# A cross-network kernel: first factors by TensorE, products on GpSimd, four head chunks, M read by quarters

## The chip, the cores and the metric

The kernel runs on one core of one Trainium2 chip. TensorE multiplies matrices into PSUM, VectorE (DVE in the profile) and GpSimd (POOL) work elementwise, ScalarE (ACT) applies functions and copies, and transfers are issued from the queues of SyncE (SP) and ScalarE. The metric is the device time of the whole kernel in microseconds (us).

## The reference

The input x has 1024 samples, 64 fields f and 16 components e. Three layers are formed, each from products of x with the layer before:

```python
z = einsum('bfe,bge->bfge', x0, h)          # all products of fields
y = einsum('oc,bce->boe', W[i], z) + b[i]   # 128 outputs
# layers 0 and 1: first 64 outputs are kept, last 64 become the next h
# layer 2: all 128 outputs are kept
out = sum_e(concat(kept)) @ fc_w.T + fc_b   # one number a sample
```

Because the last step is linear, the kernel never forms layer 2. With V2 = the row fc_w of layer 2 times W2 (64 x 64), and M = V2 applied to the last 64 outputs of W1 (a 64 x 64 x 64 tensor), layer 2 gives, for each sample and e, the sum over o of h1[o] times q[o], where h1 is the last half of layer 0 and q[o] is the sum over f and f' of M[f, f', o] x[f] x[f']. Both h1 and q are quadratic forms of the same products of x. The kept halves of layers 0 and 1 come in through small matrices called v0 and v1.

## The kernel before

**Tiles.** The samples are cut into 32 chunks of 32 samples, 512 columns each. The products of x with itself make 16 tiles of 128 rows by 512 columns, tile t = 4 j + i. Tile (j, i) is xa (the rows shifted by i) times xb (the rows shifted by 4 (j + 1), by 16 more in the lower half). `product(c, j)` makes the four tiles of one j in one VectorE instruction, 2048 elements in each partition, into a z tile. One last tile holds squares and x itself.

**Weights.** `w_all` holds, for each tile, 64 columns for h1, 64 for q, and 64 for h1 again. A full chunk takes 16 matmuls with 128 weight columns (`contract`), a product of q and h1 on VectorE (`factors`), and a sum over e (`sums`).

**Head chunks.** M is not an input: it is computed on the chip from W2 (w2s, pv, pt, v2t) and W1 (w1s, pm), copied to m_sb, written to DRAM (md) and read back along diagonals into ms. Until then only h1 can be computed. The chunks in `HEAD` therefore go through TensorE in two parts: part 0 (h1, kept in hb by `keep_h1`), and part 1 (q) when M is there. Each part multiplies 64 weight columns with the two halves of a chunk side by side (`half_contract`). The list is [4, 5, 6, 0, 1]; the products of 4, 5 and 6 are made a second time for part 1, those of the last two (`KEPT`) stay in their buffers.

**Shared last tiles.** From chunk `FIRST` = 8 on, four chunks share what follows their 16 tiles: `contract_shared` adds the squares, the v1 term and the v0 term (ys, two PSUM tiles for two pairs of chunks). Chunks below `FIRST` have a last tile each (`contract_last`), and the v0 term of a pair comes from `v0x(k)`. VectorE then multiplies it with x in `x_v0x(k)`.

**Order.** The schedule is by hand: every engine runs its instructions in the order in which the program writes them. In the main loop, turn s first loads chunk s + 2 of `order` and makes its products, then contracts chunk s, then has factors and sums of chunks before. Before the loop stand the preparation of v1 and v0 (`weigh`, two VectorE instructions of 2048 elements each).

**Buffers.** z tiles: 12 (three chunks). xa and xb: 3 each. PSUM [...]by tag: acc 4, y 2, set 2. A new tile of a tag waits until all uses of the tile that it replaces are done.

**Transfers.** Chunk loads, weights and most of M's reads are issued in order on SP; a share of M's writes and reads on ScalarE's queue.

Of the kernel before, what the change touches and what calls it, by code (L numbers as in the profile page):

```python
# [41 lines left out]
F = 64  # L42
# [6 lines left out]
NI = 4  # L49
# [4 lines left out]
HEAD = [4, 5, 6, 0, 1]  # L54
# [3 lines left out]
FIRST = 8  # L58
# [4 lines left out]
def cin_kernel(ctx, tc, xra, xrb, xh, wh, w0r, w1h, w2t, wx1, wx0, vec, out):  # L63
# [33 lines left out]

    pick = const_tile("pick", [128, 4])
# [14 lines left out]
    bd = const_tile("bd", [128, 128])  # L113
    nc.gpsimd.memset(w_all[:, NT, :], 0.0)
    nc.gpsimd.memset(bd, 0.0)


    xas, xbs, zls, xxs = {}, {}, {}, {}
# [12 lines left out]
    def load_chunk(c):  # L131
        load_xa(c)
        xb = xp.tile([128, NJ, N], F32, tag="xb", name=f"xb_{c}")
        nc.sync.dma_start(out=xb, in_=xrb[c])
        xbs[c] = [xb[:, j, :] for j in range(NJ)]

    c0, c1, c2, c3, c4 = HEAD
    xb0 = z_tile("xb0")
# [3 lines left out]
    load_xa(c0, slice(0, 2))  # L142
    nc.sync.dma_start(out=xb0[:, 0, :], in_=xh)
    load_xa(c0, slice(2, 4))
    nc.sync.dma_start(out=w0t[:, 0, :], in_=wh)
    nc.sync.dma_start(out=xb0[:, 1:NJ, :], in_=xrb[c0][:, 1:NJ, :])
    nc.sync.dma_start(out=w0t[:, 1:NJ, :], in_=w0r)
    xbs[c0] = [xb0[:, j, :] for j in range(NJ)]
    w0s = [w0t[:, j, :].rearrange("p (i v g) -> p i v g", v=2, g=F) for j in range(NJ)]
    load_chunk(c1)  # L150
    for k in range(2):
        nc.sync.dma_start(out=w2s[k], in_=w2t[k])
    load_chunk(c2)
    nc.sync.dma_start(out=w1s, in_=w1h)
# [17 lines left out]
    def product(c, j, pieces=1):  # L172
        zs[c, j] = z_tile(f"z_{c}_{j}")
        n = NI // pieces
        for i in range(0, NI, n):
            nc.vector.tensor_tensor(  # L176
                zs[c, j][:, i : i + n, :], xas[c][:, i : i + n, :],
                xbs[c][j].unsqueeze(1).to_broadcast([128, n, N]), ALU.mult,
            )
        if j == NJ - 1:  # L180
            nc.scalar.activation(zs[c, j][SQ, 0, :], xas[c][SQ, 0, :], AF.Square)  # L181
# [5 lines left out]
    def last_tile(c):  # L187

        if c < FIRST:
            squares(c)  # L190
            nc.scalar.copy(zls[c][64:128], xas[c][64:128, 0, :])  # L191
        else:
            if c % 4 == 0:
                zls[c // 4] = xp.tile([128, N], F32, tag="zl", name=f"sq_{c}", bufs=4)
            at = 32 * (c % 4)
            nc.scalar.activation(zls[c // 4][at : at + 32], xas[c][0:32, 0, :], AF.Square)  # L196
        if c % 2 == 0:
            xxs[c // 2] = sp.tile([128, N], F32, tag="xx", name=f"xx_{c}", bufs=4)
        to = halves[c % 2]
        nc.scalar.copy(xxs[c // 2][to], xas[c][to, 0, :])  # L200
# [3 lines left out]

    def pieces(c):

        return parts[c] if c in parts else [(accs[c], slice(0, N))]

    def contract(c, j, piece=0):
        acc_c, cols = pieces(c)[piece]  # L210
        for i in range(NI):
            t = j * NI + i
            nc.tensor.matmul(  # L213
                acc_c, w_all[:, t, w_cols(c)], zs[c, j][:, i, cols],
                start=(t == 0 and (c < FIRST or c % 4 < 2)),
                stop=(t == NT - 1 and c >= FIRST and c % 4 >= 2),
            )

    def contract_last(c):
        nc.tensor.matmul(accs[c], w_all[:, NT, 0:128], zls[c], start=False, stop=True)  # L220

    def contract_shared(first):

        for r in range(4):
            c, at = first + r, slice(32 * r, 32 * r + 32)
            for acc_c, cols in pieces(c):
                nc.tensor.matmul(  # L227
                    acc_c, w_sq[at, w_cols(c)], zls[first // 4][at, cols], start=(r >= 2),
                    stop=(r < 2), tile_position=(32 * r, 0),
                )  # L230
        for k in (first // 2, first // 2 + 1):
            ys[k] = ps.tile([128, N], F32, tag="y", name=f"y_{k}")
            for n in range(2):
                c, rows, q = 2 * k + n, halves[n], halves[1 - n]
                for acc_c, cols in pieces(c):
                    nc.tensor.matmul(  # L236
                        acc_c[q], v1w[rows], xxs[k][rows, cols], start=False, stop=(c % 4 < 2),
                        skip_group_check=True,
                    )
            for rows in halves:  # L240
                nc.tensor.matmul(ys[k][rows], bd[rows, rows], xxs[k][rows], start=True, stop=True)  # L241
# [3 lines left out]
    def half_contract(c, part, j):  # L245

        cols = slice(part * F, (part + 1) * F)
        rows = slice(0, F) if part == 0 and j == NJ else slice(0, 128)
        for t in (NT,) if j == NJ else range(j * NI, (j + 1) * NI):
            z = zls[c] if t == NT else zs[c, j][:, t % NI, :]  # L250
            for n in range(2):
                nc.tensor.matmul(  # L252
                    accs[c][halves[n]], w_all[rows, t, cols], z[rows, n * H2 : (n + 1) * H2],
                    start=(t == 0), stop=(t == NT),
                )
# [9 lines left out]
    def factors(c, which=slice(0, 1)):  # L265
# [9 lines left out]
        h = halves[c % 2 if c >= FIRST else 0]  # L275
# [23 lines left out]
    def h1_weights(j):  # L299
        nc.vector.tensor_tensor(  # L300
            w_all[:, j * NI : (j + 1) * NI, 0:64], w0s[j][:, :, 0, :], w0s[j][:, :, 1, :], ALU.add
        )
# [4 lines left out]
    for j in range(NJ):  # L307
        product(c0, j, 2 if j == 0 else 1)
        if j == NJ - 1:
            nc.vector.memset(w0s[j][SQ, 0, 1, :], 0.0)  # L310
        h1_weights(j)
    nc.vector.tensor_copy(w_all[0:32, NT, 0:64], w0ds[0:32])
    for j in range(NJ + 1):
        half_contract(c0, 0, j)
    keep_h1(c0)
    squares(c1)
    load_chunk(c3)

# [12 lines left out]


    new_acc(c1, H2)
    for j in range(NJ - 1):
        product(c1, j)
    for j in range(2):
        half_contract(c1, 0, j)
# [6 lines left out]
    product(c1, NJ - 1)  # L344
    half_contract(c1, 0, 2)
    load_chunk(c4)
# [11 lines left out]
    for m in range(NI):  # L358
        nc.scalar.copy(m_sb[:, m, :], pms[m])  # L359

    for j in range(3, NJ + 1):
        half_contract(c1, 0, j)
# [29 lines left out]
    def head(c):  # L392
        new_acc(c, H2)
        for j in range(NJ):
            product(c, j)
        for j in range(NJ + 1):
            half_contract(c, 0, j)
        keep_h1(c)

    head(c2)  # L400


# [7 lines left out]
    for half in range(2):  # L410
        (nc.sync, nc.scalar)[half].dma_start(
            out=ms[halves[half], 0].rearrange("p (j i) g -> p j (i g)", i=NI),
            in_=skewed(16 * half + 4, 0, [[4 * row, NJ], [1, NI * F]]),
        )
    for i in range(NI):
        for half in range(2):
            queue = nc.scalar if half and i < 2 else nc.sync
            queue.dma_start(
                out=ms[halves[half], 1].rearrange("p (j i) g -> p j i g", i=NI)[:, :, i, :],
                in_=skewed(i, 16 * half + 4, [[4 * F, NJ], [1, F]]),  # L420
            )
# [4 lines left out]
    head(c3)  # L426


    new_acc(c4, H2)
    for j in range(NJ - 1):  # L430
        product(c4, j)
        half_contract(c4, 0, j)
    nc.vector.tensor_tensor(w_all[:, 0:NT, 64:128], ms[:, 0], ms[:, 1], ALU.add)
    nc.vector.tensor_copy(w_all[SQ, (NJ - 1) * NI, 64:128], dg[SQ])
    nc.vector.tensor_copy(w_all[0:32, NT, 64:128], w_sq[0:32, 64:128])
    product(c4, NJ - 1)
    load_chunk(2)
    w1x = flat_tile("w1x")
    nc.sync.dma_start(out=w1x, in_=wx1)
# [3 lines left out]
    for j in range(NJ - 1, NJ + 1):  # L443
        half_contract(c4, 0, j)
    keep_h1(c4)
    new_acc(c4, H2)
    for j in range(NJ):
        half_contract(c4, 1, j)
# [9 lines left out]
    last_tile(2)  # L458
    for j in range(NJ):
        product(2, j)  # L460
# [10 lines left out]
    load_chunk(3)  # L471
# [19 lines left out]
    last_tile(3)  # L491
    for j in range(NJ):
        product(3, j)
# [23 lines left out]
    order = list(range(2, NCH))  # L517
    first, last = slice(0, NP - 1), slice(NP - 1, NP)
    for s, c in enumerate(order):
        k, shared = c // 2, c >= FIRST  # L520
# [6 lines left out]
        if not shared or c % 4 < 2:  # L527
            new_acc(c, H2 if c in HEAD else N)
        for j in range(NJ):
            if j == 2:  # L530
# [5 lines left out]
                if c % 2 and not shared:  # L536
                    v0x(k)
            if c in HEAD:
                half_contract(c, 1, j)
            else:  # L540
                contract(c, j)
        if c in HEAD:
            half_contract(c, 1, NJ)
        elif not shared:
            contract_last(c)
# [8 lines left out]
        elif not shared or c % 4 in (0, 3):  # L554
            factors(order[s - 1])
        elif c % 4 == 2:
# [3 lines left out]
            x_v0x(k)  # L560
        if s == 1:
            x_v0x(0)
            sums(0)
        if c % 2 and not shared:
            x_v0x(k)
        elif s and c % 2 == 0:
            sums(k - 1)
# [89 lines left out]
```

## Time and profile before

| what | value |
|---|---|
| device time, median of 3 runs (lowest, highest) | 500.45 us (500.45, 500.82) |
| span of the profiled execution | 498.6 us |
| TensorE busy | 483.2 us, 97% |
| VectorE busy | 382.3 us, 77% |
| ScalarE busy | 92.7 us, 19% |
| GpSimd busy | 1.4 us |
| DMA | 82.80 MB, mean 166 GB/s |
| TensorE, full chunks (line 213) | 896 records, 374.2 us |
| TensorE, head chunks (line 252) | 640 records, 74.1 us |
| products (line 176) | 141 instructions, 315.1 us, mean 2271 ns |

An fp32 matmul leaves two records. Timeline lines give the start, the duration, the engine, the line of the code, the operation, what is written and read, the count of instructions merged, and in brackets the idle time before and what ended it. In lines of waits the waiting instruction stands left of the arrow, then come the total, the number of times and the longest. Lines of the chain give a start, a duration and the work.

### The profile page before, as it was taken

The page shows a single profiled execution, that of the slowest core. Times are in us where ns is not written, and L with a number is a line of the kernel's source. Part 1 is how long each engine was busy: PE and PEld are TensorE (multiplying, and loading weights), DVE is VectorE, ACT ScalarE, POOL GpSimd, SP SyncE. Part 2 cuts the span into 40 slices and gives each one's busy share as a digit, 9 for nine tenths or more (in the row PEclk, how much of TensorE's full clock was granted, in tenths as well). Part 3 has the DMA queues.
Part 4 walks back from the last instruction along what each step waited for, and adds up shares of the span by engine and source line. Part 5 has one row for each costly group of instructions (what it writes and reads, how often), then busy time and mean ns, then how long its engine had stood idle before and what let it go on. Part 6 is the DMA issues. An engine that isn't in the chain of part 4 may idle for free.

```text
span 498.6 us, 4414 instructions
## 1 busy us (share of the span) xinstructions
PE 483.2 (97%) x1850; PEld 229.3 (46%) x1850; DVE 382.3 (77%) x235; ACT 92.7 (19%) x160; POOL 1.4 (0%) x14
## 2 busy tenths in 40 slices
PE   3899999999999999999999999999999999999996
PEld 1455654456444344443444434443444434444474
DVE  4999799988999889798777686776877777771311
ACT  1243033122111121322011121110111120110001
POOL 1000000000000000000000000000000000000000
PEclk9999999999999999999999999999999999999999
DMA  8997895253454444456144442333444431000000
GB/s 328 425 418 227 335 423 212 108 231 135 181 229 183 170 174 162 168 179 256 71 169 170 168 168 104 114 138 150 168 170 168 163 120 55 0 0 0 2 0 0
DMA packets 14788, 82.80 MB, mean 166 GB/s; under 512 B 3789, under 2 KB 4461, under 8 KB 5233
## 3 DMA queue, kind: packets, MB, share of 16 engines
q1 hardware_dynamic: 13644, 81.24, 41.5%
q10 hardware_dynamic: 1124, 1.29, 0.9%
q8 instruction: 14, 0.23, 0.2%
q14 instruction: 6, 0.04, 0.0%
HBM read 80.88 MB, written 1.64 MB: 165 GB/s over the span
## 4 chain that ended last, share of the span: by engine, by line
PE 91%; DMA 5%; ACT 1%; SPq 0%; ACTq 0%; issue 0%; DVE 0%
PE acc L213 75%; PE acc L252 11%; DMA w1s<-in_w1h 4%; PE acc L236 2%; DMA xb<-in_xrb 1%; PE acc L227 1%; PE y L285 1%; PE acc L220 1%; PE po L507 0%; PE pm L354 0%; ACT zl L185 0%; ACT zl L191 0%; ACT m_sb L359 0%; ACT xx L200 0%; ACTq L378 0%
## 5 line engine op out<-in xcount | busy, mean ns | idle before, releaser
L213 PE MATMUL acc<-z,w_all 128*128 128x512 f32 (+1 forms) x896 | 374.2, 578 | 0.0
L176 DVE TENSOR_TENSOR z<-xa,xb 128x2048 f32<-128x2048 f32 (+1 forms) x141 | 315.1, 2271 | 50.7 <-PE acc L213 39.5
L213 PEld LDWEIGHTS acc<-z,w_all 128*128 128x128 f32 x896 | 169.4, 190 | 202.1 <-issue 200.0
L252 PE MATMUL acc<-z,w_all 128*64 128x256 f32 x640 | 74.1, 387 | 10.7 <-DVE w_all L300 9.1
L181 ACT ACTIVATE z<-xa 32x512 f32<-32x512 f32 x35 | 21.9, 626 | 323.6 <-DVE z L176 323.6
L279 DVE SCALAR_TENSOR_TENSOR uu<-acc,vs,q 64x512 f32<-64x512 f32 (+1 forms) x28 | 20.5, 731 | 61.5 <-ACT q L278 61.3
L252 PEld LDWEIGHTS acc<-z,w_all 128*64 128x64 f32 x640 | 45.6, 139 | 39.1 <-DVE w_all L300 10.3
L278 ACT COPY q<-acc 64x512 f32<-64x512 f32 (+1 forms) x28 | 15.8, 564 | 36.4 <-PE acc L213 22.9
L292 DVE TENSOR_REDUCE acc<-uu 128x64 f32<-128x1024 f32 (+3 forms) x19 | 20.3, 1073 | 0.4
L200 ACT COPY xx<-xa 64x512 f32<-64x512 f32 x32 | 19.6, 613 | 0.4
L196 ACT ACTIVATE sq<-xa 32x512 f32<-32x512 f32 x24 | 15.1, 628 | 0.6
L241 PE MATMUL y<-xx,bd 64*64 64x512 f32 x48 | 11.7, 604 | 0.0
L288 DVE SCALAR_TENSOR_TENSOR uu<-y,cx,xx 128x512 f32<-128x512 f32 x16 | 11.4, 745 | 0.3
L236 PE MATMUL acc<-xx,v1w 64*64 64x512 f32 (+1 forms) x50 | 11.6, 584 | 0.0
L227 PE MATMUL acc<-sq,w_sq 32*128 32x512 f32 (+1 forms) x50 | 6.8, 620 | 0.0
L185 ACT ACTIVATE zl<-xa 64x512 f32<-64x512 f32 x11 | 6.8, 624 | 0.1
L236 PEld LDWEIGHTS acc<-xx,v1w 64*64 64x64 f32 x50 | 3.1, 132 | 7.5 <-issue 7.4
L252 PE MATMUL acc<-zl,w_all 64*64 64x256 f32 (+1 forms) x40 | 6.1, 393 | 0.0
L258 ACT ACTIVATE hb<-acc,vs 128x256 f32<-128x256 f32 x5 | 2.4, 474 | 19.6 <-PE acc L252 19.6
L191 ACT COPY zl<-xa 64x512 f32<-64x512 f32 x8 | 4.9, 616 | 0.1
L227 PEld LDWEIGHTS acc<-sq,w_sq 32*128 32x128 f32 x50 | 2.2, 183 | 4.6 <-issue 4.5
L271 DVE TENSOR_TENSOR uu<-acc,hb 64x256 f32<-64x256 f32 x10 | 4.2, 421 | 0.2
(52 smaller groups left out, 51.0 us busy)
## 6 DMA issues: line engine op xcount, KB each, us to landing
xa<-in_xra SPq DMA_DIRECT2D x34, 1024.0 KB, 4.8
xb<-in_xrb SPq DMA_DIRECT2D x34, 1024.0 KB, 7.0
w<-in_w2t SPq DMA_DIRECT2D x2, 1024.0 KB, 13.4
xa<-in_xra SPq DMA_DIRECT2D x2, 512.0 KB, 4.0
w1s<-in_w1h SPq DMA_DIRECT2D x1, 1024.0 KB, 20.5
w1x<-in_wx SPq DMA_DIRECT2D x1, 1024.0 KB, 8.7
w0x<-in_wx SPq DMA_DIRECT2D x1, 1024.0 KB, 10.4
xb<-in_xrb SPq DMA_DIRECT2D x1, 768.0 KB, 6.8
```

Source lines behind the costliest of these rows:

```text
L176: nc.vector.tensor_tensor(zs[c, j][:, i : i + n, :], xas[c][:, i : i + n, :], xbs[c][j].unsqueeze(1).to_broadcast([128, n, N]), ALU.mult,)
L181: nc.scalar.activation(zs[c, j][SQ, 0, :], xas[c][SQ, 0, :], AF.Square)
L196: nc.scalar.activation(zls[c // 4][at : at + 32], xas[c][0:32, 0, :], AF.Square)
L200: nc.scalar.copy(xxs[c // 2][to], xas[c][to, 0, :])
L213: nc.tensor.matmul(acc_c, w_all[:, t, w_cols(c)], zs[c, j][:, i, cols], start=(t == 0 and (c < FIRST or c % 4 < 2)), stop=(t == NT - 1 and ...
L227: nc.tensor.matmul(acc_c, w_sq[at, w_cols(c)], zls[first // 4][at, cols], start=(r >= 2), stop=(r < 2), tile_position=(32 * r, 0),)
L236: nc.tensor.matmul(acc_c[q], v1w[rows], xxs[k][rows, cols], start=False, stop=(c % 4 < 2), skip_group_check=True,)
L241: nc.tensor.matmul(ys[k][rows], bd[rows, rows], xxs[k][rows], start=True, stop=True)
L252: nc.tensor.matmul(accs[c][halves[n]], w_all[rows, t, cols], z[rows, n * H2 : (n + 1) * H2], start=(t == 0), stop=(t == NT),)
L278: nc.scalar.copy(q[h, cols], acc_c[64 - h.start : 128 - h.start])
L279: nc.vector.scalar_tensor_tensor(uu[:, cols], acc_c[h], bh1[h], q[h, cols], ALU.add, ALU.mult)
L292: nc.vector.tensor_reduce(acc[rows, of, k, half], uus[k][rows, of, E * half.start : E * half.stop].rearrange("p k (b e) -> p k b e", e=E), ...
```

## The change

- **First chunk.** `HEAD` becomes [2, 3, 0, 1] and `FIRST` 4. The first chunk's xb is no longer loaded: TensorE makes its four shifted copies from xa's tile 0 with a 0/1 matrix `shift`, built on GpSimd by three affine_selects, into PSUM tiles of tags y, y, set and acc. Six matmuls on zeros run before. xa's first load is one tile, then three.
- **Operands in PSUM.** The second factors of the first two chunks, and one operand of two weight sums (w0p), lie in PSUM. ScalarE makes the copies (`to_psum`).
- **GpSimd** makes one z tile of the first chunk (j = 1) and one of the second (j = 3).
- **Order of loads.** w1s is loaded before the third chunk. Chunk 4 is loaded behind M's reads.
- **Order of work.** The second chunk's quarters run j = 0, 3, 1, 2 among the M work. In j = 3 tile 0 comes last. m_sb is filled in the order 0, 2, 1, 3.
- **M.** ms is read in 16 transfers by quarters (12 on SP, 4 on ScalarE's queue), where there were 10; the q columns of `w_all` are summed quarter by quarter (`q_weights`), and part 1 of chunk 0 begins after the first.
- **Loop.** The order is [4, 5, 6, 7, 2, 3, 8, ...]. Chunks 4 to 7 share their last tiles; `contract_last` is gone. `sums` is called at other places. w1x lies in the buffer of ms.

```diff
-HEAD = [4, 5, 6, 0, 1]
+HEAD = [2, 3, 0, 1]
-FIRST = 8
+FIRST = 4
...
+    pw = ps.tile([128, 128], F32, tag="y", name="pw")
+    for k in range(6):
+        nc.tensor.matmul(pw, bd, bd, start=True, stop=True)
+    shift = const_tile("shift", [128, 96])
+    nc.gpsimd.memset(shift, 0.0)
+    for base in (0, 64, -64):
+        nc.gpsimd.affine_select(
+            out=shift, in_=shift, compare_op=ALU.not_equal, fill=1.0, base=base,
+            pattern=[[-1, 96]], channel_multiplier=1,
+        )
...
-    load_xa(c0, slice(0, 2))
-    nc.sync.dma_start(out=xb0[:, 0, :], in_=xh)
-    load_xa(c0, slice(2, 4))
+    load_xa(c0, slice(0, 1))
+    load_xa(c0, slice(1, 4))
     nc.sync.dma_start(out=w0t[:, 0, :], in_=wh)
-    nc.sync.dma_start(out=xb0[:, 1:NJ, :], in_=xrb[c0][:, 1:NJ, :])
     nc.sync.dma_start(out=w0t[:, 1:NJ, :], in_=w0r)
-    load_chunk(c1)
+    load_xb(c1)
+    load_xa(c1)
     for k in range(2):
         nc.sync.dma_start(out=w2s[k], in_=w2t[k])
+    nc.sync.dma_start(out=w1s, in_=w1h)
     load_chunk(c2)
-    nc.sync.dma_start(out=w1s, in_=w1h)
...
+    xbs[c0] = [
+        ps.tile([128, N], F32, tag=tag, name=f"xp_{c0}_{j}", bufs=4 if tag == "acc" else 2)
+        for j, tag in enumerate(("y", "y", "set", "acc"))
+    ]
+    for j in (0, 2):
+        for r in range(2):
+            for h in range(2):
+                at = 4 * (j + r + 1) + 16 * h
+                nc.tensor.matmul(
+                    xbs[c0][j + r][halves[h]], shift[halves[r], at : at + F],
+                    xas[c0][halves[r], 0, :], start=True, stop=True,
+                )
...
-        for i in range(NI):
+        for i in tiles(j):
...
     new_acc(c0, H2)
     squares(c0)
-    for j in range(NJ):
-        product(c0, j, 2 if j == 0 else 1)
-        if j == NJ - 1:
-            nc.vector.memset(w0s[j][SQ, 0, 1, :], 0.0)
-        h1_weights(j)
     nc.vector.tensor_copy(w_all[0:32, NT, 0:64], w0ds[0:32])
+    product(c0, 0, 0, 1)
+    product(c0, 0, 1, NI)
+    nc.scalar.copy(xb0, xbs[c0][1])
+    xbs[c0][1] = xb0
+    product(c0, 1, engine=nc.gpsimd)
+    w0p = ps.tile([128, 2, NI, F], F32, tag="set", name="w0p")
+    for j in range(2):
+        nc.scalar.copy(w0p[:, j], w0s[j][:, :, 1, :])
+    h1_weights(0, w0p[:, 0])
+    product(c0, 2)
+    h1_weights(1, w0p[:, 1])
+    h1_weights(2)
+    nc.vector.memset(w0s[3][SQ, 0, 1, :], 0.0)
+    h1_weights(3)
+    for j, tag in enumerate(("y", "y", "acc")):
+        xbs[c1][j] = to_psum(xbs[c1][j], tag, f"xp_{c1}_{j}")
+    product(c0, 3)
     for j in range(NJ + 1):
         half_contract(c0, 0, j)
+    for j in range(NJ - 1):
+        product(c1, j)
+    product(c1, NJ - 1, engine=nc.gpsimd)
     keep_h1(c0)
     squares(c1)
     load_chunk(c3)
...
-    for half in range(2):
-        (nc.sync, nc.scalar)[half].dma_start(
-            out=ms[halves[half], 0].rearrange("p (j i) g -> p j (i g)", i=NI),
-            in_=skewed(16 * half + 4, 0, [[4 * row, NJ], [1, NI * F]]),
-        )
-    for i in range(NI):
+    for j in range(NJ):
         for half in range(2):
-            queue = nc.scalar if half and i < 2 else nc.sync
+            queue = nc.scalar if half and j < 2 else nc.sync
+            to = ms[halves[half]].rearrange("p v (j i) g -> p v j i g", i=NI)
             queue.dma_start(
-                out=ms[halves[half], 1].rearrange("p (j i) g -> p j i g", i=NI)[:, :, i, :],
-                in_=skewed(i, 16 * half + 4, [[4 * F, NJ], [1, F]]),
+                out=to[:, 0, j], in_=skewed(16 * half + 4 * (j + 1), 0, [[1, NI * F]])
+            )
+            queue.dma_start(
+                out=to[:, 1, j], in_=skewed(0, 16 * half + 4 * (j + 1), [[row, NI], [1, F]])
             )
...
-    head(c3)
-    new_acc(c4, H2)
+    load_chunk(FIRST)
+    keep_h1(c2)
+    new_acc(c3, H2)
+    for j in range(NJ):
+        product(c3, j)
+        if j == 2:
+            q_weights(0)
     for j in range(NJ - 1):
-        product(c4, j)
-        half_contract(c4, 0, j)
-    nc.vector.tensor_tensor(w_all[:, 0:NT, 64:128], ms[:, 0], ms[:, 1], ALU.add)
+        half_contract(c3, 0, j)
+    new_acc(c2, H2)
+    half_contract(c2, 1, 0)
+    for j in range(NJ - 1, NJ + 1):
+        half_contract(c3, 0, j)
+    keep_h1(c3)
+    for j in range(1, NJ):
+        q_weights(j)
...
+    last_tile(FIRST)
+    for j in range(NJ):
+        product(FIRST, j)
+    w1x = set_tile("w1x")
+    nc.sync.dma_start(out=w1x, in_=wx1)
+    for j in range(1, NJ):
+        half_contract(c2, 1, j)
     new_acc(c3, H2)
     for j in range(NJ):
         half_contract(c3, 1, j)
...
-    order = list(range(2, NCH))
+    order = [4, 5, 6, 7, 2, 3] + list(range(8, NCH))
...
-        if not shared or c % 4 < 2:
+        if head or c % 4 < 2:
...
-        elif not shared:
-            contract_last(c)
         elif c % 4 == 1:
             for n in (1, 2):
                 new_acc(c + n)
             contract_shared(c - 1)
...
         if s == 1:
             x_v0x(0)
             sums(0)
```

## The prediction

> **What bounds the kernel now.** I read the page's shares and slices first, then the timelines of TensorE, VectorE and the SP queue, then the chain. The profiled execution has a span of 498.6 us; its device time was 500.42, so I add 1.85 us to a span (the other runs: 500.45 to 500.82).
>
> ```profile
> PE 483.2 (97%) x1850; PEld 229.3 (46%) x1850; DVE 382.3 (77%) x235; ACT 92.7 (19%) x160; POOL 1.4 (0%) x14
> ...
> PE   3899999999999999999999999999999999999996
> ...
> DVE  4999799988999889798777686776877777771311
> ```
>
> TensorE is the bound nearly everywhere, but in the first 14 slices (170 us) VectorE is about as full as TensorE. There a delay of VectorE can reach TensorE.
>
> ```profile
> 8.35 3.56 PE L252 MATMUL acc<-z,w_all 128*64 128x256 f32 x16 [8.35 <-DVE w_all L300]
> 12.10 1.95 PE L252 MATMUL acc<-z,w_all 128*64 128x256 f32 x16 [0.20 <-DVE w_all L300]
> ```
>
> TensorE starts at 8.35; its first quarter (one j of a head chunk) takes 3.56, the next ones 1.95. After 40.35 it never waits until the tail.
>
> ```profile
> 104.80 10.94 PE acc L252 x100
> ...
> 143.82 27.46 PE acc L213 x64
> 171.29 1.07 PE acc L227 x8
> ```
>
> From these lines of the chain: a record of a head chunk costs 10.94 / 100 = 0.109, so one part of 64 records 7.0, with its last tile 7.44. A full chunk is 27.46 / 2 = 13.73. The shared end of four chunks (L227, L236, L241) runs from 171.29 to 174.24: 2.95.
>
> ```profile
> 58.76 8.90 DVE L176 TENSOR_TENSOR z<-xa,xb 128x2048 f32<-128x2048 f32 x4 [3.14 <-DMA xb<-in_xrb]
> 67.57 2.29 DVE L454 TENSOR_TENSOR w1x<-w1x,vs 128x2048 f32<-128x2048 f32 x1
> ...
> 87.29 8.90 DVE L176 TENSOR_TENSOR z<-xa,xb 128x2048 f32<-128x2048 f32 x4
> 96.22 1.75 DVE L271 TENSOR_TENSOR uu<-acc,hb 64x256 f32<-64x256 f32 x4
> 97.99 8.90 DVE L176 TENSOR_TENSOR z<-xa,xb 128x2048 f32<-128x2048 f32 x4
> ...
> 108.86 0.73 DVE L288 SCALAR_TENSOR_TENSOR uu<-y,cx,xx 128x512 f32<-128x512 f32 x1
> ```
>
> The reader is to see one unbroken chain: from the landing of the first full chunk (58.76) VectorE runs through the products of four chunks and two weighings to x_v0x(0), done at 109.6. TensorE's next use of that y buffer is v0x(2), at 115.67, so nothing waits for it now.
>
> ```profile
> SPq L123 <- ACT z L181: 60.4, 6, 13.4
> ```
>
> This line of SP's waits shows the rule of the buffers: a tile in a used slot waits for the last reader of the tile before it (here a chunk load for ScalarE's last read of an older xa).
>
> ```profile
> 43.79 0.65 SPq L411 DMA_DIRECT2D ms<-md  x1
> 44.49 5.11 SPq L418 DMA_DIRECT2D ms<-md  x6
> 49.65 0.61 SPq L423 DMA_DIRECT2D dg<-md  x1
> 50.74 0.59 SPq L424 DMA_DIRECT2D w_sq<-md  x1
> 51.45 0.40 SPq L123 DMA_DIRECT2D xa<-in_xra  x1
> ```
>
> M's reads hold SP from 43.79 to 51.33; the chunk load behind them starts at 51.45, its second half is issued at 51.90 and lands 6.7 later, at 58.6. That is what releases the VectorE chain above.
>
> **What the Trainium skill says.** "SBUF — State Buffer", Who interferes with whom: a VectorE instruction with at most one SBUF input does not contend with GpSimd. So a factor in PSUM lets GpSimd multiply beside VectorE; no run here shows it yet, POOL now only sets memory. "PSUM — Partial Sum Buffer", Engine vs sequencer instructions: VectorE's and ScalarE's queues are strict FIFO. The trace agrees: x_v0x(0) starts at 108.86, behind chunk 5's products, as written. "TensorE: Matmul & The Clock Gate", Part 1: after an idle window of about 3.4 us the array runs at half rate until it was busy about as long; 3.56 against 1.95 agrees. Price: "GPSIMD Engine Reference", 3.1, gives 4497 ns for an fp32 tensor_tensor of 2048 elements.
>
> **The change, part by part.**
>
> *Loads.* Landings now fit 3.6 us plus bytes at 0.41 MB per us (wh 7.4, w0r 11.3). By that, afterwards: xa's first quarter about 4.4, its rest 6.3, wh 7.0, w0r 8.9, the second chunk 13.9, w2 18.9, w1s 21.5 (now 9.41 + 20.5 = 29.9). Ahead of the third chunk 1 MB leaves (xb of the first) and 1 MB enters (w1s), so it still releases VectorE at 27.46. The fourth takes the place of now 17.47 + 14.9 = 32.4.
>
> *First chunk.* The eight shift matmuls have the shape of L354 (16 records, 1.95 us). The three affine_selects are not in the trace: 0.1 us each like POOL's memsets at the low end, 2 us at the high. Behind them in POOL's queue stands the memset of w_all, for which VectorE's first copy waits. I take all as done by 4.4. Then: product of tile 0 from about 5.8, three tiles until 8.4, h1_weights(0) 8.85. So TensorE starts at 8.9, no earlier than now, but warm from the dummy matmuls (gain 0 to 1.6). GpSimd's product starts after ScalarE's copy (6.9) and ends at 11.4. A PSUM operand costs little (0.745 for 512 elements in L288), so I keep 2.21 per product: VectorE is done at 14.7, and TensorE at 17.4 (now 20.0).
>
> *Second chunk.* TensorE: four quarters 7.0, last tile 0.58, pv 2.2, pt 1.9, pm 1.9, to 31.0; pm ends at 28.6, and M is copied by 30.0 (now 33.54). VectorE ends at 21.5 and idles until 27.46, so what GpSimd saves it here is not used. GpSimd's product (13.9 to 18.4) is hidden behind this chunk's first quarter and pv.
>
> *M.* Its writes are issued from 30.0 to 32.8, with the fourth chunk ahead until 32.4. Now they ended 2.4 after the load ahead of them (41.4 to 43.79); a shorter overlap makes it 3.4: 35.8 (bounds 34.8, last issue plus 2, and 38). Reads: SP issues 12 in place of 7, then dg and w_sq. Issues back to back repeat every 0.66, so 14 take 9.2; now, with waits for earlier reads, nine took 7.54, 0.84 each, so 11.7. I take that one: 47.5. ScalarE's four stand behind chunk 0's last square (37.0), two of them for q_weights(0), there about 43.4; VectorE comes there at 42.95 (27.46 + 7 x 2.21), and behind it waits one product. The last quarter, near 51, is needed at 52.2. TensorE is held by VectorE's 42.95; from there one quarter 1.75, chunk 0's second-part quarter 1.75, the last quarter and tile 2.35, three quarters 5.25, a part 7.0, the small pcx and pc 0.4, less 0.04 of rounding: full chunks can start at 61.4 (now 72.4).
>
> The load of chunk 4 is queued on SP behind all 14: issued at 47.5, landed 7.15 later (as from 51.45 to 58.6), so 54.7; 52.2 without the waits between reads.
>
> *Work of TensorE.* One head chunk (15.0), three full chunks with a last tile (3 x 14.6) and two v0x (1.7), 60.5 in all, become a group of four: 2 x 27.46 + 2.95 = 57.9. Saved: 2.6. From 61.4 without waits: chunk 4 with the kept chunks' last tiles 14.95, chunk 5 with v0x 14.6, shared end 2.95: 93.9. Behind it: 6 and 7 27.46; second parts of 2 and 3 7.44 + 8.49 (one v0x); 8 and 9 27.66; shared 2.95; and 498.6 - 174.24 = 324.4 as now: 398.4. Without a new wait the span would be 492.3.
>
> *The new wait.* Turn s=1 is now a single chunk; afterwards it is chunk 5, which ends in contract_shared(4) with two new y tiles. Tag y has two PSUM buffers (bufs=2 of pool ps). v0x(0) of the same turn holds one until x_v0x(0), which is written behind this turn's products of chunk 7. So the second y waits on VectorE's queue, and every later chunk of TensorE is behind it. VectorE from 54.7: products of chunk 4 8.9, weighing and copies 5.4, chunk 5 8.8, weighing and copies 5.5, chunk 6 8.9, factors of the kept two 1.8, chunk 7 8.9, x_v0x 0.75; sum 49.0, so 103.7. The accumulators of 6 and 7, which wait for those factors (94.0), are free earlier. The last group of the shared end takes 0.9: 104.6. TensorE, there about 95.8, idles 7.9. A cold array after it costs 0 to 1.7; I take 1.6, the excess at the start now, since the idle is over twice 3.4. Span 104.6 + 398.4 + 1.6 = 504.6, time 506.4. Later turns are covered: chunk 8's products end near 140, TensorE comes to it at 148.
>
> *At nothing:* the tile order in j=3 (chunk 3's square of 0.63 is hidden by three tiles), sums moved (VectorE ahead of TensorE there), w1x in the set buffer (lands about 58, used at 63.6), sqs apart (names only).
>
> **Rivals.**
> A, *no wait for y*, the slot being free sooner or VectorE's order another: then the factors of the kept chunks decide, 94.0 + 0.9 + 1.9 = 96.8; span 495.2, time 497.0, faster. For it: before shows no wait on y. Against: bufs=2 and the written order. It decides if x_v0x(0) ends before about 96.
> B, *M's quarters arrive early*: VectorE's own floor for chunk 4's products is 42.95 + 0.4 + 2.25 + 1.7 = 47.3; span 47.3 + 49.0 + 0.9 + 398.4 = 495.6, time 497.5. Against: fourteen issues on SP. With the cold array, no change means a landing near 48.7.
> C, *slow GpSimd or late shift*: 4 us on the first chunk move pm, M and the load alike: time about 510.
>
> **Numbers.** Forecast, its own range 503 to 508.6, 0.70; A 0.15; B 0.05; C 0.06; a milder wait near no change 0.04. Faster 0.20, same 0.04, slower 0.76; 0.2% is 1.0 us, about what a measurement of this kernel can tell. The range 496.8 to 508.8 leaves out C and the edges.
>
> **What would show it.** Right: TensorE waiting 6 to 10 us between 93 and 106 for VectorE's x_v0x; chunk 4's products starting at 53 to 57; pm ending at 27 to 30; M's reads, dg and w_sq holding SP 10 to 12 us; a POOL product of 4 to 5 us. Wrong: no TensorE wait over 3 us between 60 and 110, or chunk 4's products before 50.

## The result and the profile after

The changed kernel takes 509.0 us (median of 6 runs, 508.65 to 510.38) against 500.45 before: ratio 1.0172, interval 1.0159 to 1.0185. It is slower by 8.6 us. The forecast was slower by 5.9, to 506.4; the measured time lies 0.2 us above the top of the stated range. The mechanism is the one forecast; one term on the way to it was too small.

First the waits of TensorE in the first 130 us (who waits, for whom, total, times, longest), from the kernel after:

```profile
PE y L275 <- DVE uu L322: 6.7, 1, 6.7
PE acc L286 <- ACT w_all L520: 2.6, 1, 2.6
PE acc L286 <- DVE w_all L334: 2.2, 1, 2.2
```

The first line is the wait for the y buffer: TensorE's second y matmul (line 275) for VectorE's x_v0x (line 322). It is the longest wait of TensorE in the kernel. The second is a wait that the prediction did not name: the last tiles of the kept chunks need v1's weights, which VectorE weighs behind chunk 4's products. It costs nothing here: without it TensorE would only come 2.6 us earlier to the longer wait, whose end VectorE sets.

Next TensorE's timeline around it, then VectorE's from chunk 4 on:

```profile
98.22 1.02 PE L270 MATMUL acc<-xx,v1w 64*64 64x512 f32 x4
105.90 1.97 PE L275 MATMUL y<-xx,bd 64*64 64x512 f32 x4 [6.66 <-DVE uu L322]
107.80 17.60 PE L251 MATMUL acc<-z,w_all 128*128 128x512 f32 x39
```

```profile
57.13 8.90 DVE L210 TENSOR_TENSOR z<-xa,xb 128x2048 f32<-128x2048 f32 x4 [5.36 <-DMA xb<-in_xrb]
...
96.17 8.90 DVE L210 TENSOR_TENSOR z<-xa,xb 128x2048 f32<-128x2048 f32 x4
105.10 0.75 DVE L322 SCALAR_TENSOR_TENSOR uu<-y,cx,xx 128x512 f32<-128x512 f32 x1
```

VectorE runs without a gap worth the name from the landing of chunk 4's factors (57.13) to x_v0x(0), done at 105.85; 0.05 us later TensorE moves. The matmuls of y take 1.97 where the same group takes 1.07 when the array has just been at work (e7 below); the clock that the trace shows as granted is 0.50 from 102.2 to 109.0. The first line of VectorE's timeline also shows where its chain starts: after 5.36 us of idle time, on a chunk load.

What stands ahead of that load on SP:

```profile
31.27 0.52 SPq L424 DMA_DIRECT2D md<-m_sb  x1
...
34.38 2.00 SPq L430 DMA_DIRECT2D md<-m_sb  x1
39.85 0.47 SPq L459 DMA_DIRECT2D ms<-md  x1
...
49.21 0.61 SPq L467 DMA_DIRECT2D w_sq<-md  x1
49.93 0.40 SPq L135 DMA_DIRECT2D xa<-in_xra  x1
```

M's writes begin at 31.27, its reads at 39.85, chunk 4's load at 49.93. All three are in one queue and in one chain. The chain that ended last confirms it; in order of time (start, duration, work):

```profile
50.38 6.63 DMA xb<-in_xrb
...
57.13 8.90 DVE z L210 x4
...
105.10 0.76 DVE uu L322
105.90 1.97 PE y L275 x4
```

### The profile page after: what moved, and what is told of

Read it like the earlier page. It is cut to its first block, busy times and chain, and to the rows that moved or that the text cites. A ratio compares the mean times of both kernels' runs of the same rounds, so it can differ in the third digit from the quotient of the medians.

```text
span 507.0 us, 4297 instructions
## 1 busy us (share of the span) xinstructions
PE 490.6 (97%) x1788; PEld 229.9 (45%) x1788; DVE 370.3 (73%) x231; ACT 92.8 (18%) x161; POOL 11.4 (2%) x20
## 4 chain that ended last, share of the span: by engine, by line
PE 84%; DVE 9%; DMA 3%; SPq 2%; issue 1%; ACT 0%; DVEq 0%; ACTq 0%
PE acc L251 71%; PE acc L286 8%; DVE z L210 7%; PE acc L270 2%; DMA xb<-in_xrb 1%; PE acc L261 1%; DMA w0t<-in_w0r 1%; SPq L462 1%; SPq L459 1%; PE y L275 1%; DVE v1h L512 0%; DVE v0h L512 0%; DVE w0x L511 0%; DVE w1x L511 0%; PE po L561 0%
## 5 line engine op out<-in xcount | busy, mean ns | idle before, releaser
L251 PE MATMUL acc<-z,w_all 128*128 128x512 f32 (+1 forms) x928 | 389.0, 580 | 0.0
L210 DVE TENSOR_TENSOR z<-xa,xb 128x2048 f32<-128x2048 f32 x128 | 289.0, 2287 | 60.3 <-PE acc L251 48.9
L251 PEld LDWEIGHTS acc<-z,w_all 128*128 128x128 f32 x928 | 176.2, 191 | 211.7 <-issue 209.9
L286 PE MATMUL acc<-z,w_all 128*64 128x256 f32 x512 | 59.3, 389 | 2.2 <-DVE w_all L334 2.2
L286 PEld LDWEIGHTS acc<-z,w_all 128*64 128x64 f32 x512 | 36.7, 140 | 26.1 <-issue 5.2
L275 PE MATMUL y<-xx,bd 64*64 64x512 f32 x56 | 14.7, 639 | 6.7 <-DVE uu L322 6.7
L230 ACT ACTIVATE sq<-xa 32x512 f32<-32x512 f32 x28 | 17.6, 628 | 5.2 <-DMA xa<-in_xra 4.5
L210 DVE TENSOR_TENSOR z<-xa,xp 128x2048 f32<-128x2048 f32 (+2 forms) x7 | 13.5, 1976 | 1.7 <-PE xp L185 1.7
L322 DVE SCALAR_TENSOR_TENSOR uu<-y,cx,xx 128x512 f32<-128x512 f32 x16 | 11.4, 746 | 0.3
L210 POOL TENSOR_TENSOR z<-xa,xb 128x2048 f32<-128x2048 f32 x2 | 9.1, 4552 | 5.7 <-ACT xb L345 3.4
L275 PEld LDWEIGHTS y<-xx,bd 64*64 64x64 f32 x56 | 3.2, 137 | 7.5 <-DVE uu L322 7.5
```

The lines of the kernel that those rows point to most:

```text
L210: engine.tensor_tensor(zs[c, j][:, at, :], xas[c][:, at, :], xbs[c][j].unsqueeze(1).to_broadcast([128, last - first, N]), ALU.mult,)
L230: nc.scalar.activation(sqs[c // 4][at : at + 32], xas[c][0:32, 0, :], AF.Square)
L251: nc.tensor.matmul(acc_c, w_all[:, t, w_cols(c)], zs[c, j][:, i, cols], start=(t == 0 and c % 4 < 2), stop=(t == NT - NI and c % 4 >= 2),)
L286: nc.tensor.matmul(accs[c][halves[n]], w_all[rows, t, cols], z[rows, n * H2 : (n + 1) * H2], start=(t == 0), stop=(t == NT),)
```

## The experiments

Three theories were set against each other. *The y buffer*: TensorE waits for x_v0x(0) because a y tile has no free buffer, and the time follows, one to one, whatever moves VectorE's arrival there; that arrival follows chunk 4's landing. *The backlog*: VectorE is so late that squares, accumulators or products would hold TensorE anyway. *M or the start*: the loss is M's lateness, however the y buffer is arranged. Each experiment edits the changed kernel.

**e1: x_v0x(0) ahead of chunk 7's products.**

```diff
             last_tile(ahead)
-            for j in range(NJ):
-                product(ahead, j)
+            if s != 1:
+                for j in range(NJ):
+                    product(ahead, j)
...
                 if s == 1:
                     v0x(0)
+                    x_v0x(0)
+                    sums(0)
+                    for jj in range(NJ):
+                        product(ahead, jj)
...
-        if s == 1:
-            x_v0x(0)
-            sums(0)
```

> Only the written order on VectorE changes in turn s=1: x_v0x(0) and sums(0) stand before the products of chunk 7. Theory of the y buffer: TensorE's 6.7 us wait for VectorE's L322 goes, and so does the half-rate restart after it; contract(6) starts near 99.2 in place of 107.8, span about 497.6, time 499 to 500.5. Rival, VectorE's backlog alone (squares, accumulators or products of chunk 7 would hold TensorE anyway): another wait takes its place, gain under 2.5 us, time 506.5 to 509.

Measured: 499.84 us, ratio to before 0.9988 (0.9981 to 0.9995). The same two instructions in another place are worth 9.2 us, more than the whole loss. M was no earlier (its writes begin at 31.78, against 31.27), so M's lateness alone is not the loss. The wait for L322 is gone from the list of waits; TensorE's timeline of e1:

```profile
94.86 3.05 PE L261 MATMUL acc<-sq,w_sq 32*128 32x512 f32 x8
...
99.72 12.71 PE L251 MATMUL acc<-z,w_all 128*128 128x512 f32 x29
```

Chunk 6 starts at 99.72 (107.80 in the changed kernel). The squares take 3.05 where 1.14 is their time elsewhere: about 1.9 us of waiting, for the accumulators that the kept chunks' factors release (these run from 94.94 to 96.68 on VectorE). So the backlog theory holds for 1.9 us (and the 2.6 for v1), and the y buffer for the rest. This also says what the change without its new wait was worth: practically nothing.

**e2: chunk 4's load between M's writes and M's reads; e3: e1 and e2 together.**

```diff
+    load_chunk(FIRST)
     keep_h1(c1)
     squares(c2)
...
-    load_chunk(FIRST)
```

> Only the load of chunk 4 moves on SP, from behind M's reads to between M's writes and M's reads. Theory of the queue (chunk 4's landing sets VectorE, VectorE sets the y wait): products of chunk 4 start at 52 to 55 in place of 57.1, and the time falls by as much, 504 to 507. Rival, M itself is the limit (reads are slowed by the 2 MB by as much as the load gains): no gain, 508.5 to 510.

> The two edits of e1 and e2 together. Theory of the y buffer: TensorE is nearly without waits, span 493.5 to 496, time 495.5 to 498, under both kernels. Rival, backlog: as e2, 504 or more.

Measured: e2 511.18 us (ratio 1.0212, 1.0196 to 1.0227); e3 503.05 (1.0046, 1.0029 to 1.0062). Both missed. SP's queue and VectorE's timeline of e2 show why:

```profile
39.31 0.35 SPq L145 DMA_DIRECT2D xb<-in_xrb  x1
40.05 0.47 SPq L460 DMA_DIRECT2D ms<-md  x1
...
49.80 0.45 SPq L460 DMA_DIRECT2D ms<-md  x1
```

```profile
50.32 0.42 DVE L472 TENSOR_TENSOR w_all<-ms 128x256 f32<-128x256 f32 x1 [7.62 <-DMA ms<-md]
...
57.91 8.88 DVE L210 TENSOR_TENSOR z<-xa,xb 128x2048 f32<-128x2048 f32 x4
```

The load is in time, but M's first quarter stands behind its 2 MB: VectorE waits 7.62 us for it, and chunk 4's products, which the program writes behind all sums of M's quarters, start at 57.91, no earlier. TensorE waits 5.4 us for the quarter too. In e2 it then comes later to the y wait, which ends at 106.67 (105.90); the rest of e2's loss is the clock, as the table under e7 shows. A load put in front of another in one queue gave its delay to that one, here to the more urgent. In e3 this wait remains (5.3 us), while the y wait is gone: e3 is slower than e1 by 3.2.

**e10: chunk 4's load behind that of the fourth head chunk (chunk 1), ahead of all of M's transfers.**

```diff
     load_chunk(c3)
+    load_chunk(FIRST)
...
-    load_chunk(FIRST)
```

> As the changed kernel, but the load of chunk 4 stands on SP right behind that of the fourth chunk, ahead of all of M's transfers. Theory of the queue: it lands before 42, M's writes end 1 to 2 us later (they share the engines with 2 MB), VectorE goes from the last copy of M's weights (near 53) straight to the products of chunk 4, 3 to 4 us earlier than 57.1: time 505 to 506. Rival (M is delayed by as much as in e2): no gain.

Measured: 505.91 (1.0105, 1.0091 to 1.0119). As expected, chunk 4's products start earlier, at 52.90 (57.13), although M's reads begin later, at 41.50 (39.85). x_v0x(0) ends 4.2 us earlier, and TensorE waits for it as before, 6.2 us. The span of the profiled run, its fastest, follows by 3.8 and the median time by 3.1. This is the y theory's forecast: the same wait, moved with its releaser. The table under e7 shows what is missing to one to one.

**e6: M's reads in ten transfers, as in the kernel before.** The two loops of transfers were put back; the sums by quarters stayed.

```diff
-    for j in range(NJ):
-        for half in range(2):
-            ...
+    for half in range(2):
+        (nc.sync, nc.scalar)[half].dma_start(
+            out=ms[halves[half], 0].rearrange("p (j i) g -> p j (i g)", i=NI),
+            in_=skewed(16 * half + 4, 0, [[4 * row, NJ], [1, NI * F]]),
+        )
+    for i in range(NI):
+        ...
```

> M's reads as in the kernel before (10 transfers, 7 of them on SP); the sums stay by quarters. Theory of the queue: chunk 4's load is issued 2 to 3 us earlier, so the time falls to 506 to 507, although TensorE must wait 3 to 5 us more for the first quarter of M near 44. Rival (M's first quarter decides): slower by those 3 to 5 us, 512 to 514.

Measured: 506.85 (1.0120, 1.0103 to 1.0137), 2.2 us under the changed kernel. Two lines of TensorE's waits in e6:

```profile
PE y L275 <- DVE uu L322: 4.5, 1, 4.5
...
PE acc L286 <- DVE w_all L475: 3.4, 1, 3.4
```

TensorE now waits 3.4 us for M's first quarter, and 2.2 less for y. The quarters do bring part 1 forward, and TensorE then waits that time later: the five more issues on SP cost more than they bring, as long as the y wait stands. The profile alone would overstate this: of the 1.9 us by which chunk 4's products start earlier (55.22), about 0.6 come from M itself, whose reads begin at 39.23 (39.85), since the first chunk ran at full clock in this run (see the cold array below).

**e4 and e5: each of GpSimd's two products back on VectorE.**

```diff
-    for j in range(NJ - 1):
-        product(c1, j)
-    product(c1, NJ - 1, engine=nc.gpsimd)
+    for j in (0, 3, 1, 2):
+        product(c1, j)
```

```diff
-    product(c0, 1, engine=nc.gpsimd)
+    product(c0, 1)
```

> The second chunk's product j=3 goes back from GpSimd to VectorE (VectorE in the order 0, 3, 1, 2). VectorE idles 5.5 us before 27.2 there, so theory: no change, 508.5 to 509.5, VectorE's idle time before 27.2 shrinks to about 3.3. If the help mattered: 2 us slower, 511.

> The first chunk's product j=1 goes back from GpSimd to VectorE. Theory: TensorE starts and ends the first chunk 1.5 to 2 us later, pm, M's writes and reads and the load of chunk 4 move as much, time 510.5 to 511. If the writes of M or the fourth load set M alone: no change, 508.5 to 509.5.

Measured: e4 510.58 (1.0197, 1.0180 to 1.0213; runs from 509.44 to 511.56), e5 513.34 (1.0248, 1.0213 to 1.0283). In e4's profile all that matters stays or moves a little forward: VectorE idles 3.70 us before the third chunk (5.49), x_v0x(0) ends at 105.5, TensorE waits 6.7. So the help is not used. The interval overlaps that of the changed kernel, so the 1.6 us between the medians are not shown to be the product's. The clock is the likelier cause: the profiled run is the fastest, with a mean granted clock of 0.992, and the other three have 0.981 to 0.986. e5 is a miss by size: 4.3 us, not 2. Its four runs stand in two pairs, 511.08 and 511.98, 514.71 and 514.77, and the profile is of the slowest. Its VectorE timeline, then GpSimd's:

```profile
13.40 0.42 DVE L334 TENSOR_TENSOR w_all<-w0t 128x256 f32<-128x256 f32 x1
...
14.04 4.61 DVE L334 TENSOR_TENSOR w_all<-w0t 128x256 f32<-128x256 f32 x1
```

```profile
13.85 4.52 POOL L210 TENSOR_TENSOR z<-xa,xb 128x2048 f32<-128x2048 f32 x1 [10.43 <-DMA xa<-in_xra]
```

The same sum of weights takes 0.42 at 13.40 and 4.61 at 14.04, to the end of GpSimd's product. Both of its operands lie in SBUF. The Trainium skill, "SBUF — State Buffer", Who interferes with whom, says that a VectorE instruction with two inputs in SBUF contends with a GpSimd instruction that reads SBUF, and that the ports which the two share are an exclusive lock; the 4.61 us beside GpSimd's 4.52 agree. In the changed kernel the same sum runs at 12.51, before GpSimd's second product at 13.63: the order avoids it by 0.7 us. Behind it M's writes begin 4.5 us later, at 35.81, and chunk 4's products 5.0 later, at 62.16. In e5 GpSimd's product starts only 0.2 us ahead of the sum that it holds up. Whether the faster pair of runs escaped the collision is open.

**e8: a small write of M ahead of the large ones; e9: the large writes cut in four.**

```diff
+    nc.sync.dma_start(out=m_ap(64, 64, [[row, 32], [1, 4 * F]]), in_=m_rows[0:32, 0 : 4 * F])
     for half, queue in enumerate((nc.sync, nc.scalar)):
...
-    nc.sync.dma_start(out=m_ap(64, 64, [[row, 32], [1, 4 * F]]), in_=m_rows[0:32, 0 : 4 * F])
```

```diff
-        queue.dma_start(
-            out=m_ap(0, 32 * half, [[row, F], [1, 32 * F]]), in_=m_rows[halves[half]]
-        )
+        for m in (0, 2, 1, 3):
+            queue.dma_start(
+                out=m_ap(0, 32 * half + 8 * m, [[row, F], [1, 8 * F]]),
+                in_=m_sb[halves[half], m, :],
+            )
```

> The write of md rows 64 to 95 by columns 64 to 67 (it needs only the first quarter of m_sb, and its issue took 1.9 us of SP) goes ahead of the large writes. If the chain of issues sets the end of M's writes: reads begin 1.5 to 2 us earlier (38 in place of 39.85) and the time falls as much, 507 to 507.5. If the large writes' own transfer sets it (7 us from issue to landing): no change.

> The two large writes of M (512 KB each, rows of 8 KB) are cut into four each (rows of 2 KB), issued as each quarter of m_sb is copied, from about 29.8 on. In every run so far the reads of M began 8.4 to 8.6 us after the first write, wherever that was. If the writes' own transfer takes that time, an earlier start brings the reads 1 to 1.5 us forward, and the time as much: 507.5 to 508. If more transfers only make the queue longer: reads at 40 or later, 509 to 510.

Measured: e8 510.44 (1.0193, 1.0178 to 1.0208), e9 508.55 (1.0170, 1.0141 to 1.0200). In e8 the last write is issued by 34.8 (36.4 in the changed kernel), yet reads begin at 40.08: the issues on SP do not set the end of the writes. The 1.4 us by which e8 is slower are the clock's in its profile: the y wait ends only 0.3 later, but the half clock after it lasts 2.9 us longer (table under e7). In e9 reads begin at 38.21, 1.6 us earlier, and chunk 4's products 1.4 earlier (55.72); the median gains only 0.5, which is within its scatter (507.23 to 511.1). What the engines did while the changed kernel wrote M, a microsecond at a time (behind the window come the busy times of PE, PEld, DVE, ACT and POOL, the granted clock, the share of the DMA engines and GB/s):

```profile
33.00:34.00 1.00, 1.00 (x12) 0.67 (x10) 1.00 (x2) 0.88 (x2) 0.00 (x0) 1.00 1.23 254
34.00:35.00 1.00, 1.00 (x14) 0.64 (x12) 1.00 (x1) 0.99 (x3) 0.00 (x0) 1.00 0.73 131
```

Over 32 to 39 the mean is 231 GB/s, with a DMA share of 0.57 to 1.23; from 24 to 30 the loads ran at 410 to 418. M's 1.6 MB of writes take 7 us at 231 GB/s by themselves. Why the writes are slower is not settled.

**e7: TensorE kept busy in the wait.**

```diff
         for k in (first // 2, first // 2 + 1):
+            if k == 3:
+                warm = ps.tile([128, N], F32, tag="set", name="warm")
+                for _ in range(7):
+                    nc.tensor.matmul(warm, bd, xxs[k], start=True, stop=True)
             ys[k] = ps.tile([128, N], F32, tag="y", name=f"y_{k}")
```

> Seven dummy matmuls of 128x128x512 (0.86 us each, 6.0 us) fill TensorE's wait for the y buffer; their result is not used. If the half rate after the idle time costs what the first 3 us after it suggest, the span falls by 1.5 to 2, time 507 to 507.5. If the array had not cooled, or the wait's end is not what starts it, no change: 508.5 to 509.5.

Measured: 507.44 (1.0137, 1.0121 to 1.0152), 1.6 us under the changed kernel, with 6.3 us of useless work added:

```profile
98.51 6.28 PE L269 MATMUL warm<-xx,bd 128*128 128x512 f32 x14
...
106.09 1.07 PE L279 MATMUL y<-xx,bd 64*64 64x512 f32 x4 [0.30 <-DVE uu L326]
```

The Trainium skill, "TensorE: Matmul & The Clock Gate", Part 1, says that an idle array falls to half rate. The traces agree: the granted clock is 0.50 after the y wait of the changed kernel, and 1.00 throughout from 76 to 505 in e7. The table has every profile in which x_v0x(0) stands where the changed kernel has it: when TensorE resumes with the y matmuls, until when the clock then stays at 0.50, the rest of the span, and that rest less half of the time at 0.50.

| run | resumes | 0.50 until | rest of the span | less half of the 0.50 |
|---|---|---|---|---|
| changed kernel | 105.90 | 109.04 | 401.1 | 399.5 |
| e2 | 106.67 | 112.54 | 402.5 | 399.6 |
| e4 | 105.54 | 110.58 | 402.1 | 399.5 |
| e5 | 110.94 | 115.90 | 402.1 | 399.6 |
| e6 | 104.00 | 107.03 | 401.0 | 399.5 |
| e7 | 106.09 | none | 399.6 | 399.6 |
| e8 | 106.19 | 112.24 | 402.6 | 399.6 |
| e9 | 104.50 | 109.17 | 402.0 | 399.7 |
| e10 | 101.66 | 105.51 | 401.5 | 399.6 |

So two things account for the span of all nine to 0.2 us: when the y wait ends, one to one, and how long the clock stays at half. The second cost 1.5 to 3.0 us for waits of 4.5 to 6.7, and not in the order of their length.

**b1 and b2: a version from these.** b1 joins e1 and e10 and makes chunk 4's first two products between the sums of M's quarters; b2 adds e9.

```diff
+    last_tile(FIRST)
     for j in range(1, NJ):
         q_weights(j)
+        if j < NJ - 1:
+            product(FIRST, j - 1)
...
-    last_tile(FIRST)
-    for j in range(NJ):
+    for j in range(2, NJ):
         product(FIRST, j)
```

> e1 and e10 together, and VectorE makes the first two products of chunk 4 between the sums of M's quarters. VectorE is then ahead by some 8 us, so TensorE has no wait from 65 on but the accumulators: span 493 to 495.5, time 495 to 497.5, under both kernels. If the head's order costs TensorE as much (a wait for M's quarters near 45 to 53): 498 to 500.

> b1 with the writes of e9. TensorE needs M near 45, so an earlier M by 1 us gives 0 to 1 us over b1: 494.5 to 497.5; if e9's cut makes M later, 0.5 to 1 us over b1.

Measured: b1 495.92 us, ratio to before 0.9915 (0.9902 to 0.9927), under both kernels. TensorE's timeline, from its slowest run (497.53):

```profile
94.15 1.14 PE L261 MATMUL acc<-sq,w_sq 32*128 32x512 f32 x8
...
97.10 7.13 PE L251 MATMUL acc<-z,w_all 128*128 128x512 f32 x16
```

The squares take 1.14 again, y is not waited for, and chunk 6 starts at 97.10; the wait for v1's weights is gone from the list as well. b2, at 503.82 (1.0066, 1.0054 to 1.0079), is a miss. On ScalarE's queue:

```profile
32.66 6.76 ACTq L426 DMA_DIRECT2D md<-m_sb  x3
...
44.57 0.62 ACT L215 ACTIVATE z<-xa 32x512 f32<-32x512 f32 x1
```

Three of the small writes hold ScalarE's queue for 6.76 us, with 2 MB of loads ahead of them in the engines (401 to 455 GB/s from 30 to 35), and the square that a z tile of chunk 0 needs comes at 44.57; TensorE waits 5.9 us for it. In e9, with the same cut, the engines moved only 107 to 119 GB/s from 30 to 32; three writes held the queue for 2.44 us, and M's reads began earlier.

## Why the prediction was right and wrong

- *The new wait.* Right in place, cause and direction: the wait at 99 to 106 for x_v0x, 6.7 us where 6 to 10 were forecast. e1 shows it by its removal. VectorE's chain was summed to 49.0 us and took 48.7. Chunk 4's products, at 57.13, came just behind the 53 to 57 that were named as a sign.
- *The cold array.* Forecast 1.6, and half of the time at 0.50 after the wait is 1.57. The closeness is partly luck: the other profiles with this wait paid 1.5 to 3.0, where the prediction allowed 0 to 1.7. At the start it was not as forecast. After a gap of 2.2 us the clock stood at 0.50 from 10.05 to 13.47, and the first chunk's 64 records took 8.81, in spite of the dummy matmuls. In e3, e4 and e6 the same chunk ran at full clock, after gaps of 3.2 to 3.8 us, so this differs from run to run. In e4 and e6 M's writes begin at 30.5 to 30.6, in the changed kernel at 31.27: of the 1.2 us by which M was copied late (31.24, not 30.0), about 0.7 are the clock, and the rest is the start at 9.48 in place of 8.9.
- *M's writes: the step that failed.* The prediction said "a shorter overlap makes it 3.4: 35.8 (bounds 34.8, last issue plus 2, and 38)". Reads began at 39.85, outside both bounds. It timed the end of the writes from the end of the load ahead of them, as a tail of 3.4 us behind 32.4. From the copy of M to the reads this made 5.8 us; it took 8.6, and the load had already landed at about 30. The runs show a duration of the writes' own: 8.4 to 8.6 us from the first large write to the first read in the changed kernel, e1, e4, e5 and e8, wherever that write stood (31.3, 31.8, 30.5, 35.8, 31.7). The two lines below are e5's. Its engines moved nothing from 32 to 36, so no load was ahead of these writes, and they took as long.

```profile
35.81 0.52 SPq L424 DMA_DIRECT2D md<-m_sb  x1
...
44.39 0.47 SPq L459 DMA_DIRECT2D ms<-md  x1
```

- *M's reads and the load.* Forecast 11.7 us to the load's issue; it took 10.1 (39.85 to 49.93), 14 issues at 0.72. Landing after it: forecast 7.15, measured 7.2. Chunk 4's products start at 57.13, not 54.7: 1.2 late from the copy of M, 2.8 late from its writes, 1.6 early from its reads. The span, 507.0, is 2.4 over the forecast 504.6. The term of the writes alone is more than this miss, and the other two nearly cancel.
- *GpSimd.* Price 4.5, measured 4.53 and 4.58; unused for the second chunk, as forecast (e4). What no run had shown before now is: a product with a factor in PSUM takes 2.28 us on VectorE (at 9.34) beside GpSimd's product (6.79 to 11.32), where a product took 2.28 to 2.29 before.
- *The rivals.* A gave 497.0 without a y wait; e1, the chip's version of it, gives 499.84, late by about as much as chunk 4's products are in it (57.67, 3.0 behind 54.7). B did not come about, as the load was issued at 49.93. C gave about 510, nearer to the measured time than the forecast, but not by its cause: the affine_selects took 0.93 us, GpSimd its price, and the first chunk's end and pm were late by 0.9 and 1.4 us, not 4.
- *Not forecast*: the 2.6 us wait for v1's weights, harmless behind a longer one.

## What to carry to other kernels

When work moves in a hand-written order, list for every buffer of a small pool who holds it, and where its last reader stands in that reader's queue: a reader of 0.75 us written behind 8.9 us of unrelated products cost this kernel 9 us. Then follow the chain back through every queue, since five more issues ahead of a load are paid by all that waits for the load. Before a transfer is moved ahead of another, ask which of the two is the more urgent: the same load gained 3.1 us ahead of M's writes (e10) and nothing between M's writes and M's reads (e2). And count more for a wait than its length: TensorE's idle time cost a further 1.5 to 3.0 us at half clock.

## What the hardware showed that was not expected

Writes of M to DRAM ran at 231 GB/s over 7 us, against 410 to 418 for the loads from 24 to 30. A weight sum with both operands in SBUF took 4.61 us instead of 0.42 beside a GpSimd product. Three affine_selects of 128x96 took 0.93 us together. Small writes queued behind 2 MB of loads held the issuing engine for 6.76 us (three of them on ScalarE's queue in b2), so a transfer can block arithmetic on the engine that issues it. After TensorE's waits every stretch at half clock lasted 3.4, 6.8 or 10.2 us in these traces (but for those that end with the kernel), so the price of a wait varied between runs of the same code; the first chunk of the changed kernel was slowed by one in its profile and not in those of e3, e4 and e6.
